# Layer 0 transposes x in 64-row halves, the condition's weights lead SP's queue, and the list run gets the trace's durations

## The chip, the cores and the metric

The kernel runs on one core of a Trainium2 chip. The metric is the device time of one execution in microseconds (us), lower is better. The kernel before takes 1091.3 us, the median of three runs (1090.01 to 1092.24). Engines are named as in the profile: PE is TensorE's matmul, PEld its weight load, DVE is VectorE, ACT is ScalarE, POOL is GpSimd, SP is the engine that issues most of the DMAs. A name with q (SPq, ACTq) is an engine's sequencer, which issues DMAs and waits.

## The reference, cut to what matters

x is 8 x 512 x 256, the condition 8 x 64, all in float32. Two layers follow each other; each batch element is independent of the others.

```python
# layer 0
scale = cond @ norm_w.T + 1.0
h = x * (scale[:, None, :] * rsqrt(mean(x * x, -1) + EPS))
val, gate = split(h @ up_w.T, 2, axis=-1)
h = val * gelu(gate)                      # 512 x 1024
hq = round-to-127-levels(h, per row);  wq = ternary(down_w)
x = hq @ wq.T + x
# layer 1, 16 heads of 16
x = x + a_alpha * attention(gamma * rmsnorm(x) + beta)
x = x + f_alpha * swiglu(gamma' * rmsnorm(x) + beta')
```

All `gamma`, `beta` and `alpha` are products of the condition with a weight of 256 x 64. They and `norm_w` are side by side in one array, `cond_w` (64 x 1792); its first 256 columns are `norm_w`.

## The kernel before, in words

Every step of the kernel is recorded as an operation of a plan: an engine, a cost in us, a function that emits the instructions, the values that it reads and writes, and a due time `at`. `Plan.order` then runs a list schedule: it keeps a clock for each engine, and whenever an engine is free it gives it the ready operation with the smallest due time. The order that comes out is the program order of every engine and of every DMA queue. So the costs written in the code decide which instruction stands ahead of which, and nothing else; on the chip an engine works through its order and waits on semaphores where it must. A DMA issued by ACT counts in the list as an ACT operation, whose result is there 0.12 us after its end; one issued by SP is there 2.5 us after its end.

PE operations have a mode: `full` (128 x 128), `rows` (two tiles of 64 rows, used side by side: scores, row maxima, the gated transposes of layer 1) and `columns` (four tiles of 32 columns, `quarters`, L383). A change of mode has a cost in the list, and rules keep modes together for a while. Values that need PSUM take one of 8 banks, or a pair of neighbours, from a named pool: `u` is banks 0 to 3 (results of the up matmuls), `fill` is 7, 5 and 6, `tp` the pairs (5,6), (2,3), (0,1). Pools may overlap; the list hands out the slot that has been free longest.

Order of the work: the start loads x of batch 0 in two halves (L390), the up weights in eight blocks of 256 KB (`load_up`, L403), and by ACT's queue the condition (`ct`) and `norm_w` (`nw`, both L394). POOL makes constants (L435 to L438) and fills `vts` and `thirds` (L456, L457). DVE makes `pick` in `constants2` (L443 to L446), which the scores need much later. PE multiplies `nw` by `ct` (L464), DVE adds 1 and writes it to `cvec` (L471): that is the value `scale`.

`norm0` (layer 0) squares x on ACT (L653), takes the root on POOL (L661, L662) and transposes x, not normalized, on PE. For batch 0 this goes in four pieces of two 128x128 transposes (`some`, L673), and the copy out of PSUM multiplies by `scale`, on ACT for the first 128 features (L678) and on DVE for the others (L680). For batches 1 to 7 there are two groups of four 128x128 transposes (L689), each into one `fill` bank, and two copies on ACT (L694). `up_tile` does 128 tokens: matmuls of 512 columns, two for each of four results (L710), GELU on ACT (L717), product on DVE (L744), the quantization (L756 to L779), a DMA transpose (L787), the down matmuls (L795) and the residual (L804).

Six batches of layer 0 go by themselves (to about 220 us); the last two are done in `columns` mode in between the attention of the first batches. Attention takes 128 steps of 5.8 us due time each: two score groups (L915, L917), exp on ACT (L948), row maxima for a later step (L932 on PE, L941 on DVE), weighted sums (L991), with projections and the swiglu of other batches (L383) in the gaps. `split` (L967 to L970) prepares the maxima for the scores. In layer 1 the normalized x before the swiglu is already transposed by halves: 16 transposes of 64 rows, two at a time, into a `tp` pair (`halves`, L581), and copied by L591.

Of the kernel before, what the change touches and what calls it, by code (L numbers as in the profile page):

```python
# [36 lines left out]
BF16 = mybir.dt.bfloat16  # L37
# [219 lines left out]
def act(n):  # L257
    return (n / 1.2 + 125) / 1e3


def dve(n):
    return (n / 0.96 + 115) / 1e3
# [11 lines left out]
def two_layers(ctx: ExitStack, tc: tile.TileContext, x, cond_t, cond_w, up_t, down_t, qkvo_t, gh_t, out_t, out_b, out):  # L274
# [109 lines left out]


# [11 lines left out]
    load("nw", lambda: mem(V["nw"])[:C, :D], cond_w[:, :D], -88, queue=se)  # L397
# [3 lines left out]
    def load_up(c, k):  # L401
        v = wup[c, k] = Val("wup")
        op("SP", dma(256), lambda: sp.dma_start(out=mem(v), in_=up_v[:, c, k * 512 : (k + 1) * 512]), writes=[v], at=-80)  # L403
# [49 lines left out]
    op("DVE", 2.0, constants2, writes=[V["pick"]], reads=[V["const"]], at=20)  # L453
# [24 lines left out]
    op("DVE", 0.2, lambda: condition_out(pn, 0, 1), reads=[pn], writes=[V["scale"]], at=-50)  # L478
    op("PE", 3.6, lambda: condition(pc, cw(), 1, 4), reads=[V["cw"], V["ct"]], writes=[pc], at=30)
# [52 lines left out]
    def norm(src, vsrc, scale, bias, name, at, step, pool="ht", gated=False):  # L532
# [10 lines left out]
        for t in range(NT):  # L543

            def square(t=t):
                if t == 0:
                    squares()
                ve.scalar_tensor_tensor(  # L548
                    mem(xn)[:, t * D : (t + 1) * D], in0=src()[:, t, :], scalar=1.0, in1=src()[:, t, :],
                    op0=ALU.mult, op1=ALU.mult, accum_out=ssq[0][:, t : t + 1],  # L550
                )

            op("DVE", 0.43, square, reads=[vsrc[t]], writes=[vs, xn], at=at)
# [9 lines left out]
        for t in range(NT):  # L563
            op(
                "DVE", 0.35,
                lambda t=t: ve.tensor_scalar(  # L566
                    mem(xn)[:, t * D : (t + 1) * D], src()[:, t, :], rstd[0][:, t : t + 1], None, op0=ALU.mult
                ),
                reads=[vs, vsrc[t]], writes=[xn], at=at + step,
            )  # L570
        ht = Val(pool)
        if gated:

            pt = Val("tp")

            def halves():
                for c in range(NC):
                    for t in range(NT):
                        for e in range(2):
                            r = slice(64 * e, 64 * e + 64)  # L580
                            pe.transpose(  # L581
                                mem(pt)[:, e, (c * NT + t) * 64 : (c * NT + t + 1) * 64],
                                mem(xn)[r, t * D + c * P : t * D + (c + 1) * P], ident[r, r],
                            )
# [3 lines left out]
            for c in range(NC):  # L588
                op(
                    "ACT", 0.65,  # L590
                    lambda c=c: se.activation(  # L591
                        mem(ht)[:, c * S : (c + 1) * S].rearrange("p (t e q) -> p t e q", t=NT, e=2),
                        mem(pt)[:, :, c * 256 : (c + 1) * 256].rearrange("p e (t q) -> p t e q", t=NT),
                        AF.Identity, bias=bias(c), scale=scale(c),
                    ),
                    reads=[pt, V["cvec"]], writes=[ht], at=at + (2 + c) * step,
                )
            return ht
        for c in range(NC):
            pt = Val("fill")  # L600

            def transposes(c=c, pt=pt):
# [9 lines left out]
                "ACT", 0.65,  # L612
# [33 lines left out]
    def norm0(b):  # L646
# [19 lines left out]
        for n in range(4 if b == 0 else 0):  # L666

            u, c = divmod(n, 2)
            pt = Val("fill")

            def some(u=u, c=c, pt=pt):
                for t in range(2):
                    pe.transpose(mem(pt)[:, t * P : (t + 1) * P], x1[:, b, 2 * u + t, c * P : (c + 1) * P], ident)  # L673

            def scaled(u=u, c=c, pt=pt):
                o, i, w = mem(ht)[:, c * S + u * 256 : c * S + u * 256 + 256], mem(pt)[:, :256], cvec[:, 0, c, b : b + 1]
# [5 lines left out]
            op("PE", 0.4, some, reads=[*vx1[b][2 * u : 2 * u + 2], V["const"]], writes=[pt], at=at + n * step, also=[ht])  # L682
            op(("ACT", "DVE")[c], act(256), scaled, reads=[pt, V["scale"]], writes=[pieces[u][c]], at=at + n * step, also=[ht])
        for c in range(NC if b else 0):
            pt = Val("fill")

            def transposes(c=c, pt=pt):
                for t in range(NT):
                    pe.transpose(mem(pt)[:, t * P : (t + 1) * P], x1[:, b, t, c * P : (c + 1) * P], ident)  # L689

            op("PE", 0.5, transposes, reads=[*vx1[b], V["const"]], writes=[pt], at=at + (2 + c) * step, also=[ht])
            op(
                "ACT", 0.65,
                lambda c=c, pt=pt: se.activation(  # L694
                    mem(ht)[:, c * S : (c + 1) * S], mem(pt), AF.Identity, scale=cvec[:, 0, c, b : b + 1]
# [5 lines left out]
    def up_tile(b, t, ht, at, late=False):  # L701
# [56 lines left out]
        def scales():  # L758
# [7 lines left out]
        op("DVE", 1.2, top, reads=[h], writes=[vst], at=a8)  # L766
        op("DVE", 0.6, scales, reads=[V["mean"]], writes=[vst], at=a8)
        op(
            "DVE", 0.7, lambda: ve.tensor_scalar(mem(h), mem(h), st["sc"], MAGIC, op0=ALU.mult, op1=ALU.add),
# [4 lines left out]
            "ACT", act(1024), lambda: se.activation(mem(q).bitcast(BF16), mem(h), AF.Identity, bias=magic),  # L774
# [3 lines left out]
            "DVE", 0.35,  # L778
# [12 lines left out]
        def down():  # L791
# [11 lines left out]
            "DVE", 0.42,  # L803
# [99 lines left out]
    def half_step(s, p):  # L903
# [4 lines left out]
        if now is not None:  # L908
# [3 lines left out]
            def scores():  # L912
# [10 lines left out]
                "PE", 0.43, scores, reads=[val["qk", n], vshift[n % 2], V["pick"]], writes=[sc], at=at, mode="rows",  # L923
# [28 lines left out]
    def shift(m):  # L952
# [19 lines left out]
        op("DVE", 0.5, split, reads=[vtop[k]], writes=[vthird[k]], at=at)  # L972
# [114 lines left out]
    def swiglu(b, at, first, place, stride=1.0):  # L1087
# [13 lines left out]
        for f in range(NF):  # L1101
            ps = []
            t, hid, gt = Val("t"), Val("hid"), Val("gt")
            for s in range(2):
# [22 lines left out]
                "DVE", dve(512) + 0.05,  # L1127
# [132 lines left out]
```

## Time and profile before

| what | value |
|---|---|
| median of three runs | 1091.3 us |
| the profiled execution: its time, its span | 1090.63 us, 1088.9 us |
| PE busy | 1065.4 us, 98% of the span |
| DVE, ACT, POOL busy | 631.7, 518.8, 205.7 us |
| granted TensorE clock, mean | 0.999 |
| DMA | 116.93 MB, mean 107 GB/s |
| four 128x128 transposes of L689, 48 of 56 before 215 us | 0.273 us each, pipelined |
| 16 half transposes of L581, x224 in all | 0.225 us each, pipelined |

The span is the time from the first to the last instruction of the profiled execution; the remainder of its time lies around it. A busy share of PE counts pipelined matmuls once, and their ends are modelled. In the timeline each line is: start, duration, engine, line of the code, operation, output and input, count, and in brackets the idle time before it with what ended it. In the waits each line is: who waited, for what, total us, how many times, the longest. In the windows each line is a stretch with the busy time and the number of instructions of PE, PEld, DVE, ACT and POOL, then the granted clock, the DMA share and GB/s.

### The profile page before, as it was taken

What the parts mean: (1) busy time and instruction counts of PE and PEld (TensorE: products, weight loads), DVE (VectorE), ACT (ScalarE), POOL (GpSimd) and SP (SyncE); (2) the same over time, 40 slices, a digit from 0 to 9 for tenths busy, and PEclk for the clock granted to TensorE, in tenths of its full rate; (3) what the DMA queues carried; (4) which work ended last, traced back from release to release, by engine and by line L of the source; (5) the groups of instructions that cost most, each with busy time, mean ns of one, the idle gap of its engine ahead of it and who ended that gap; (6) DMA issues with size and microseconds to landing.
All of it is one profiled execution on the core that took longest, in us unless ns stands there. A gap on an engine that the chain in (4) does not pass through costs nothing.

```text
span 1088.9 us, 22177 instructions
## 1 busy us (share of the span) xinstructions
PE 1065.4 (98%) x9336; PEld 442.9 (41%) x9336; DVE 631.7 (58%) x1044; ACT 518.8 (48%) x692; POOL 205.7 (19%) x198
## 2 busy tenths in 40 slices
PE   7999999999999999999999999999999999999998
PEld 4555454433333333433443344334333433342445
DVE  5665556876666854475557556654755474553131
ACT  3434433266666554455535544554455354436321
POOL 2100000000000321131123112311321132123242
PEclk9999999999999999999999999999999999999999
DMA  6322872124534542453254225514432452311100
GB/s 193 98 68 58 232 203 59 29 62 123 130 105 112 154 131 69 126 182 104 64 181 123 88 87 170 169 55 145 138 114 65 152 153 77 102 56 46 33 18 20
DMA packets 113828, 116.93 MB, mean 107 GB/s; under 512 B 59448, under 2 KB 69880, under 8 KB 113728
## 3 DMA queue, kind: packets, MB, share of 16 engines
q1 hardware_dynamic: 113568, 115.45, 36.5%
q8 instruction: 73, 1.20, 0.5%
q14 instruction: 27, 0.22, 0.1%
q10 hardware_dynamic: 160, 0.07, 0.0%
HBM read 56.49 MB, written 46.42 MB: 95 GB/s over the span
## 4 chain that ended last, share of the span: by engine, by line
PE 89%; DVE 5%; DMA 2%; ACT 2%; issue 1%; POOL 0%; ACTq 0%; SPq 0%; DVEq 0%
PE banks L383 40%; PE banks L710 15%; PE banks L991 9%; PE banks L915 6%; PE banks L932 5%; PE banks L917 4%; PE banks L1110 3%; DVE tops L941 2%; PE banks L795 2%; DMA a<-a 1%; PE banks L1151 1%; ACT a L948 1%; DMA aq<-hld 1%; DVE a L548 1%; DVE a L566 1%
## 5 line engine op out<-in xcount | busy, mean ns | idle before, releaser
L941 DVE TENSOR_REDUCE tops<-banks 128x2 f32<-128x1024 f32 x256 | 309.8, 1222 | 160.3 <-PE banks L932 158.8
L948 ACT ACTIVATE a<-banks 128x1024 f32<-128x1024 f32 x256 | 257.3, 1024 | 170.3 <-PE banks L917 152.9
L383 PE MATMUL banks<-a,gh 128*32 128x512 f32 x1792 | 208.2, 595 | 0.0
L710 PE MATMUL banks<-a,a 128*128 128x512 f32 x384 | 173.2, 599 | 0.4 <-DVE tops L941 0.4
L917 PE MATMUL banks<-aq 64*128 64x512 f32 x512 | 148.9, 577 | 0.0
L991 PE MATMUL banks<-a,vts 128*32 128x512 f32 x1024 | 135.1, 601 | 0.0
L1138 POOL TENSOR_TENSOR a<-a 128x512 f32<-128x512 f32 x64 | 81.8, 1278 | 256.8 <-ACT a L1134 248.6
L915 PE MATMUL banks<-shifts,pick 64*128 64x512 bf16 x512 | 101.2, 386 | 7.3 <-ACT a L948 5.1
L932 PE MATMUL banks<-aq 64*128 64x512 f32 x512 | 103.5, 417 | 4.4 <-ACT a L948 2.2
L383 PE MATMUL banks<-wout,a 128*32 128x256 f32 x1792 | 107.4, 381 | 0.0
L1128 DVE SCALAR_TENSOR_TENSOR a<-a,banks 128x512 f32<-128x512 f32 x64 | 44.0, 687 | 103.2 <-ACT a L1123 103.2
L710 PEld LDWEIGHTS banks<-a,a 128*128 128x128 f32 x384 | 71.2, 192 | 78.8 <-issue 73.5
L383 PEld LDWEIGHTS banks<-a,gh 128*32 128x32 f32 x1792 | 53.5, 109 | 119.7 <-issue 109.4
L915 PEld LDWEIGHTS <-pick 64*128 64x128 bf16 x512 | 26.8, 93 | 155.9 <-issue 150.8
L744 DVE SCALAR_TENSOR_TENSOR a<-banks,rstds,a 128x512 f32<-128x512 f32 x64 | 48.0, 750 | 68.4 <-PE banks L710 54.1
L717 ACT ACTIVATE a<-banks,rstds 128x512 f32<-128x512 f32 x64 | 43.4, 686 | 85.8 <-PE banks L710 83.0
L383 PEld LDWEIGHTS banks<-wout,a 128*32 128x32 f32 x1792 | 54.8, 110 | 52.9 <-issue 23.3
L1134 ACT ACTIVATE a<-banks 128x512 f32<-128x512 f32 x64 | 38.2, 597 | 73.5 <-PE banks L383 64.5
L1123 ACT ACTIVATE a<-banks 128x512 f32<-128x512 f32 x64 | 38.2, 597 | 63.2 <-PE banks L383 43.5
L1082 POOL TENSOR_TENSOR x<-x,a 128x512 f32<-128x512 f32 x31 | 40.2, 1298 | 138.7 <-DVE a L1073 132.5
L932 PEld LDWEIGHTS banks<-aq 64*128 64x128 f32 x512 | 48.7, 186 | 38.1 <-ACT a L948 12.0
L383 PE MATMUL banks<-a,a 128*32 128x512 f32 x512 | 59.3, 595 | 0.2 <-DVE a L744 0.2
(106 smaller groups left out, 945.2 us busy)
## 6 DMA issues: line engine op xcount, KB each, us to landing
hld<-a SPq DMA_DIRECT2D x128, 256.0 KB
aq<-hld SPq DMA_DIRECT2D x64, 512.0 KB
zd<-a SPq DMA_DIRECT2D x32, 256.0 KB
a<-zd SPq DMA_DIRECT2D x16, 256.0 KB
a<-rd SPq DMA_DIRECT2D x16, 256.0 KB
out_dram<-x SPq DMA_DIRECT2D x15, 256.0 KB
x<-in_x_dram SPq DMA_DIRECT2D x7, 512.0 KB
a<-in_up_t_dram SPq DMA_DIRECT2D x8, 256.0 KB
```

Source lines behind the costliest of these rows:

```text
L383: pe.matmul(o[32 * i : 32 * i + 32, :], w[:, 32 * i : 32 * i + 32], r, start=start, stop=stop)
L710: (quarters if late else pe.matmul)(mem(us[half, j]), mem(ht)[:, c * S + t * P : c * S + (t + 1) * P], mem(wup[c, 2 * half + j]), start=c ...
L717: se.activation(mem(gs[j]), mem(us[1, j]), AF.Gelu, scale=rstds[:, b, t : t + 1])
L744: lambda v=us[0, j], g=gs[j], j=j: ve.scalar_tensor_tensor(mem(h)[:, j * 512 : (j + 1) * 512], in0=mem(v), scalar=rstds[:, b, t : t + 1], ...
L915: pe.matmul(mem(sc)[:, e, :], pick[r, p, :], shifts[r, n % 2, :], start=True, stop=False)
L917: pe.matmul(mem(sc)[:, e, :], tile_of(n, 1, p, e)[:, kc * P : (kc + 1) * P], tile_of(n, 0, p, e), start=False, stop=True,)
L932: pe.matmul(mem(pm)[:, e, :], tile_of(m, 0, p, e)[:, qc * P : (qc + 1) * P], tile_of(m, 1, p, e), start=True, stop=True,)
L941: lambda: ve.tensor_reduce(tops[:, m % 2, 2 * p : 2 * p + 2, qc], mem(pm), AX.X, ALU.max, negate=True),
L948: lambda: se.activation(mem(e).rearrange("p (i s) -> p i s", i=2), mem(sc), AF.Exp, scale=0.25),
L991: pe.matmul(mem(pa)[32 * i : 32 * i + 32, :], vts[:, b % 2, kc, 8 * c + 4 * j + i, :], mem(es[i // 2])[:, (i % 2) * S : (i % 2 + 1) * S], ...
L1128: lambda t=t, i=ps[0]: ve.scalar_tensor_tensor(mem(t), in0=mem(t), scalar=1.0, in1=mem(i), op0=ALU.add, op1=ALU.mult),
L1138: "POOL", pool(512), lambda t=t, h=hid, g=gt: gp.tensor_tensor(mem(g), mem(t), mem(h), op=ALU.mult),
```

## The change

Three things are changed. First, `norm0` transposes x by halves: a helper `turn` makes two 64-row transposes of each 128x128 block, in mode `rows`, into a `tp` pair of banks; batches 1 to 7 get one group of 16 halves in place of two groups of four, and the copies read both banks with a rearranged pattern. Second, the start: `nw` is loaded by SP ahead of x, the up block (0, 2) by ACT in the place where `nw` was, and `constants2` now reads `scale`, so that it comes after L471. Third, the costs in the list: the formulas for ACT and DVE get 45 and 40 ns more, and a dozen single costs are set anew. The code that computes is not changed by the third.

```diff
 def act(n):
-    return (n / 1.2 + 125) / 1e3
+    return (n / 1.2 + 170) / 1e3
 def dve(n):
-    return (n / 0.96 + 115) / 1e3
+    return (n / 0.96 + 155) / 1e3
...
+    def turn(o, at, i):
+
+        for e in range(2):
+            r = slice(64 * e, 64 * e + 64)
+            pe.transpose(o[:, e, at : at + 64], i[r], ident[r, r])
...
-    load("nw", lambda: mem(V["nw"])[:C, :D], cond_w[:, :D], -88, queue=se)
+    load("nw", lambda: mem(V["nw"])[:C, :D], cond_w[:, :D], -95)
     load_x(0, -90, n=2)
...
-        op("SP", dma(256), lambda: sp.dma_start(out=mem(v), in_=up_v[:, c, k * 512 : (k + 1) * 512]), writes=[v], at=-80)
+        e, queue = ("ACT", se) if c == 0 and k == 2 else ("SP", sp)
+        op(e, 0.6 if e == "ACT" else dma(256), lambda: queue.dma_start(out=mem(v), in_=up_v[:, c, k * 512 : (k + 1) * 512]),
+           writes=[v], at=-88 if e == "ACT" else -80)
...
-    op("DVE", 2.0, constants2, writes=[V["pick"]], reads=[V["const"]], at=20)
...
     op("DVE", 0.2, lambda: condition_out(pn, 0, 1), reads=[pn], writes=[V["scale"]], at=-50)
+    op("DVE", 2.0, constants2, writes=[V["pick"]], reads=[V["const"], V["scale"]], at=20)
...
         for n in range(4 if b == 0 else 0):
             u, c = divmod(n, 2)
-            pt = Val("fill")
+            pt = Val("tp")
             def some(u=u, c=c, pt=pt):
                 for t in range(2):
-                    pe.transpose(mem(pt)[:, t * P : (t + 1) * P], x1[:, b, 2 * u + t, c * P : (c + 1) * P], ident)
+                    turn(mem(pt), t * 64, x1[:, b, 2 * u + t, c * P : (c + 1) * P])
...
-            op("PE", 0.4, some, ...)
+            op("PE", 0.2, some, ..., mode="rows")
...
-        for c in range(NC if b else 0):
-            pt = Val("fill")
-
-            def transposes(c=c, pt=pt):
+        if b == 0:
+            return ht
+        pt = Val("tp")
+
+        def halves():
+            for c in range(NC):
                 for t in range(NT):
-                    pe.transpose(mem(pt)[:, t * P : (t + 1) * P], x1[:, b, t, c * P : (c + 1) * P], ident)
+                    turn(mem(pt), (c * NT + t) * 64, x1[:, b, t, c * P : (c + 1) * P])
-            op("PE", 0.5, transposes, reads=[*vx1[b], V["const"]], writes=[pt], at=at + (2 + c) * step, also=[ht])
+        op("PE", 0.62, halves, reads=[*vx1[b], V["const"]], writes=[pt], at=at + 2 * step, also=[ht], mode="rows")
...
-            "DVE", 0.7, lambda: ve.tensor_scalar(mem(h), mem(h), st["sc"], MAGIC, op0=ALU.mult, op1=ALU.add),
+            "DVE", 0.98, lambda: ve.tensor_scalar(mem(h), mem(h), st["sc"], MAGIC, op0=ALU.mult, op1=ALU.add),
...
-                "PE", 0.43, scores, reads=[val["qk", n], vshift[n % 2], V["pick"]], writes=[sc], at=at, mode="rows",
+                "PE", 0.455, scores, reads=[val["qk", n], vshift[n % 2], V["pick"]], writes=[sc], at=at, mode="rows",
...
-        op("DVE", 0.5, split, reads=[vtop[k]], writes=[vthird[k]], at=at)
+        op("DVE", 0.95, split, reads=[vtop[k]], writes=[vthird[k]], at=at)
```

The other new costs: the squares of `norm` 0.43 to 0.47, its products 0.35 to 0.4, the row maximum of a tile (L756) 1.2 to 1.22, the rounding on ACT (L774) 0.1 more, the clipping (L779) 0.35 to 0.42, the residual (L804) 0.42 to 0.48, the ACT copies after transposes 0.65 to 0.77, and the swiglu's product (L1128) loses 0.05 that it had on top of the formula. `halves` of layer 1 is written with `turn` and stays as it was.

## The prediction

> **What bounds the kernel now.** I read the page first, its busy shares and its chain of work.
>
> ```profile
> span 1088.9 us, 22177 instructions
> PE 1065.4 (98%) x9336; PEld 442.9 (41%) x9336; DVE 631.7 (58%) x1044; ACT 518.8 (48%) x692; POOL 205.7 (19%) x198
> PE 89%; DVE 5%; DMA 2%; ACT 2%; issue 1%; POOL 0%; ACTq 0%; SPq 0%; DVEq 0%
> ```
>
> TensorE (PE) has 98% and 89% of the chain; nobody else comes near. What shortens the time is a shorter PE step or a shorter PE wait. Next come the stages of the run (columns: busy time of PE, PEld, DVE, ACT, POOL, then granted clock, DMA share, GB/s).
>
> ```profile
> 13.00:220.00 207.00, 206.28 (x685) 102.58 (x684) 133.06 (x262) 80.69 (x140) 12.07 (x16) 1.00 0.43 107
> 220.00:1010.00 790.00, 777.61 (x8099) 295.64 (x8101) 474.41 (x741) 416.88 (x514) 160.28 (x143) 1.00 0.38 113
> ```
>
> Layer 0 leaves PE idle for 0.7 us of 207, attention for 12.4 of 790. Third, the timeline of the start.
>
> ```profile
> 0.72 0.97 SPq L390 DMA_DIRECT2D x<-in_x_dram  x2
> 1.30 0.61 ACTq L394 DMA_DIRECT2D a<-in_cond_w_dram  x1
> 2.04 4.08 DVE L446 TENSOR_SCALAR pick<-ones,pair 128x128 bf16<-128x128 f32 x1
> 5.51 0.52 POOL L457 MEMSET thirds<- 128x512 bf16 x1
> 6.11 0.99 PE L464 MATMUL banks<-ct,a 64*128 64x8 f32 x4 [6.11 <-DMA a<-in_cond_w_dram]
> 7.03 1.97 PE L673 MATMUL banks<-ident,x 128*128 128x128 f32 x8
> 8.79 15.64 PE L710 MATMUL banks<-a,a 128*128 128x512 f32 x32
> 10.50 0.34 PEld L710 LDWEIGHTS banks<-a,a 128*128 128x128 f32 x1 [0.52 <-issue]
> 12.68 0.19 PEld L710 LDWEIGHTS banks<-a,a 128*128 128x128 f32 x1 [0.24 <-issue]
> ```
>
> PE does nothing until 6.11: its first work is the condition (L464), and its weights, issued second on ACT's queue at 1.30, land only then. The transposes of x stand behind it in PE's order, though ACT already reads x's first half at 3.78. The first up matmul starts at 8.79; its weight loads come 0.85 us apart until 12.2 and 0.43 apart from then on: the clock is half until there.
>
> **The change, part by part**, summed against the profiled execution's own 1090.63 us (span 1088.9 and 1.7 around it); the median of the runs shown is 1091.3, so 0.7 above it.
>
> *Start.* The condition's weights (64 KB) go to the head of SP's queue, and x's two halves and seven up blocks move back by one issue there (0.43 to 0.5 us each); one up block goes to ACT's queue in the weights' old place, so ACT issues as much as before. x's first half, four times as large, is issued at 0.72 and read at 3.78; so the weights are there by 3.8 at the latest. The four condition matmuls took 0.92 (6.11 to 7.03): done at 4.7, and `scale` by DVE (0.17) at 4.9. x's first half, one issue later, lands near 4.3; its transposes run on the cold clock (0.22 for each 128x128: 8 from 7.03 to 8.79), and half tiles run two at a time, so about 0.5: done at 5.2, ACT's copy (0.47) at 5.7.
> DVE has the other half of the pieces, and here the moved `constants2` matters. It now reads `scale`, so it can start at 4.9; the list has it ready at once, while the pieces still wait for x, so I expect it ahead of them. Its first L446 ran 4.08 us and ended at 6.12, 0.09 after POOL's last memset (6.03): I take it that it can't end before 6.1 after the change either. The second pair (0.15 + 0.29) ends at 6.6, DVE's first piece (0.48) at 7.1. That piece feeds the second matmul of the first up group, now at 9.64 (8.79 + 0.85). Upper bound of the gain: 9.64 - 7.1 - 0.1 = 2.4 us. The next late thing is the up weights: in the trace's semaphore events the fourth load of 256 KB is complete at 7.93, and the same bytes are ahead of it afterwards; by that the gain is 1.7. If the clock still doubles at 12.2, the time won is spent on cold matmuls (0.85 for 0.43) and half stays, 0.9. The pieces now take pairs of banks, two of them up banks, so the first up group also waits until ACT has read the third piece: x's second half near 5.0, transposed by 5.5, two squares (0.4 each) and the copy, 6.3; earlier than the DVE piece. No loss follows from any of these rows, so the ends are 0 and -2.4. I take **-1.6**, nearest to the weights' landing.
> The row for the clock is the spacing above: 3.4 us of up matmuls until it doubles. The Trainium skill (TensorE: Matmul & The Clock Gate, Part 1) says that a busy window of about 3.4 us, free-running, opens the clock; by that an earlier start is an earlier fast clock and the term stays whole, give or take a window in single runs.
>
> *Transposes, batches 1 to 7.* Each has two groups of four 128x128 transposes now, then one group of 16 in 64-row tiles, in pairs. Layer 1 has this form already, at L581.
>
> ```profile
> 95.97 0.60 PE L689 MATMUL banks<-ident,x 128*128 128x128 f32 x4
> 96.41 3.60 PE L710 MATMUL banks<-a,a 128*128 128x512 f32 x8
> 99.84 1.04 PE L604 MATMUL banks<-ident,a 128*128 128x128 f32 x8
> ```
> ```profile
> 217.50 3.70 PE L710 MATMUL banks<-a,a 128*128 128x512 f32 x8
> 221.13 0.71 PE L581 MATMUL banks<-ident,a 64*128 64x64 f32 x16
> 221.67 0.38 PE L915 MATMUL banks<-shifts,pick 64*128 64x512 bf16 x2
> ...
> 227.91 0.40 PE L932 MATMUL banks<-aq 64*128 64x512 f32 x2
> 228.24 1.06 PE L991 MATMUL banks<-a,vts 128*32 128x512 f32 x8
> ```
>
> A step is the distance of starts, since durations overlap. Four transposes: 0.44; a batch's two groups 0.88. Sixteen halves: 221.13 to 221.67, 0.54. But the array's shape changes on both sides. Eight up matmuls between equals take 3.43 (96.41 to 99.84); those at 217.50, behind 64-row work and ahead of it, 3.63: so 0.20 for the entry into rows and the first full matmul after rows. Leaving costs the last pair 0.10 (0.33 at 227.91, where a pair inside a run takes 0.23 on the chain). Among up matmuls a batch thus costs 0.54 + 0.20 + 0.10 = 0.84 for 0.88: five batches, -0.2. Batches 6 and 7 stand among 64-row work already (188.5 and 222.5 to 227.5): there the switch goes too; 0.88 becomes 0.54, and about as much again for the switch of one of them, together -0.8. Sum **-1.0**. ACT's copies of halves are longer (L591 0.774, L694 0.685), 14 x 0.09 = 1.2 us of ACT, which is busy for 81 of 207 us: nothing. The new form needs two neighbouring PSUM banks at once. (5,6) are hardly used in layer 0; if the list took two of the up tiles' four banks, PE would wait for at most the two copies, 1.5 us a batch: 6 x 1.5 = +9 is the far end, the near one -1.0 - 0.6.
> Against this part speaks the Trainium skill (TensorEngine Tiling (Array Packing), Key Properties): changing the tiling mode drains TensorE. It gives no price; by the rule alone five batches would lose. The rows show the drain, 0.30 a round trip, and the pairs pay for it.
>
> *The list's durations.* No instruction changes, but the order on all engines is worked out anew. The large ones: exp 0.978 to 1.023 (L948 runs 1.024), row maxima 1.182 to 1.222 (L941 1.222), scores 0.43 to 0.455, splits 0.5 to 0.95 (four instructions, 0.97). One moves away: the scaling at L769 goes from 0.7 to 0.98 and runs 0.75. What can be won is PE waiting behind work that the list thought done earlier. The waits of attention (us, times, longest):
>
> ```profile
> PE banks L915 <- ACT a L948: 5.1, 5, 2.1
> PE banks L932 <- ACT a L948: 2.2, 6, 0.4
> PE banks L915 <- DVE tops L941: 1.7, 5, 0.4
> ```
>
> With the weight loads' waits, PE stands behind L948 or L941 48 times there. Each was 0.04 to 0.045 too early: 48 x 0.045 = 2.2, and I take half, since an order that avoids one wait often makes another: **-1.1**. The ends: all of PE's idle 12.4 gone, and on the other side more changes of shape. I count 218 returns from 64-row work in PE's records; entry and exit cost 0.19 to 0.30. A tenth more rounds is 22 x 0.2 = +4.4.
>
> **Sum**: 1090.63 - 1.6 - 1.0 - 1.1 = 1086.9; from the median it would be 1087.6. I say **1087.0**.
>
> **Rivals.** About 0.2% (2.2 us) is what a measurement of this kernel can tell from no change.
> (1) *Forecast*: start and transposes pay, the order is neutral to slightly better: 1083 to 1089, 0.50.
> (2) *The order gains much*: the waits behind L948 and L941 (9.6 us on PE itself in attention) mostly go: 1086.9 - 5 = 1082, reaching 1079. For it: these waits; against: the list's error is only 4%, and the waits of 1 to 2 us at 222.9 and 250 follow table loads on ACT (1.28), which no duration here changes. 0.16.
> (3) *The start is hidden*: up weights or clock take back the gain, or the change does not do what it says (DVE's first piece waits for `constants2` and POOL's memsets as long as it waited for the condition, or the durations move away as at L769): with -0.5 to -1 for the transposes, 1089.1 to 1092. 0.21.
> (4) *Slower*: the new order changes PE's shape more often. It decides when the added rounds eat the 3.7 us and 2.2 more: 5.9 / 0.2 = 30 more than 218. Then 1093.5 to 1097. For it: the longer scores and maxima can break up runs of 64-row work; against: the rules of batching are untouched. 0.13.
>
> Faster by over 0.2%: (1) and (2), 0.66; within: 0.21; slower: 0.13. The range leaves out the far part of (2) and (4): 1081 to 1093.
>
> **What would show it.** Start: condition before 4.8, L446 ending near 6.1, first up matmul between 6.2 and 8, its second before 8.3. Wrong if DVE's piece comes after 8. Transposes: 16 halves in 0.54, next up matmul within 0.7; wrong if PE waits at them for a bank. Order: PE idle in 220 to 1010 below 12 us and no more than about 218 rounds; a count beyond 240 would mean (4).

## The result, and the profile after

The changed kernel takes 1105.5 us (median of four runs, 1104.43 to 1106.4); the kernel before, in the same session, 1091.7 (median of four, 1090.01 to 1092.24). The ratio is 1.0129 with an interval of [1.0111, 1.0146]: 13.8 us slower, where I had said 4 us faster and given "slower" 0.13. The profiled execution took 1104.69 us (before 1090.63). From here on, L numbers are those of the kernel that a line is from; in the changed kernel the lines of attention stand 8 further down (L915 becomes L923, L932 L940, L941 L949, L948 L956), L710 is L718, and all half transposes are issued in `turn`, L389.

The page of the changed kernel, span, busy shares and chain:

```profile
span 1102.9 us, 22312 instructions
PE 1068.7 (97%) x9400; PEld 441.7 (40%) x9400; DVE 631.2 (57%) x1044; ACT 519.4 (47%) x692; POOL 205.3 (19%) x198
PE 89%; DMA 4%; DVE 3%; ACT 2%; issue 1%; SPq 1%; POOL 0%; DVEq 0%; ACTq 0%
```

PE is still the only engine that matters. It is busy for 3.3 us more in a span that is 14.0 longer, so most of the loss is PE waiting. The windows of the two stages (columns as in the prediction):

```profile
13.00:220.00 207.00, 205.83 (x732) 100.31 (x731) 134.29 (x261) 80.33 (x139) 11.52 (x16) 1.00 0.44 108
220.00:1010.00 790.00, 767.13 (x7986) 292.97 (x7988) 475.00 (x740) 410.59 (x504) 156.56 (x140) 1.00 0.39 113
```

Layer 0 is as full as before (1.2 us idle for 0.7). In attention PE idles 22.9 us for 12.4, and it gets through 8099 - 7986 = 113 matmuls fewer in the same 790 us. The first score of attention comes at 221.18 us in the trace (221.67 before), the last at 1021.7 (1008.0 before); what follows is as long as it was (81.2 us for 80.9). From first to last score it takes 800.5 us for 786.3. So the whole loss lies between the first and the last score. The waits of PE in the changed kernel:

```profile
PE banks L923 <- ACT a L956: 8.2, 9, 2.6
PE banks L923 <- DVE tops L949: 5.3, 8, 1.3
...
PE banks L389 <- ACT a L956: 2.8, 3, 0.9
PE banks L940 <- DVE tops L949: 1.7, 3, 0.9
...
PE banks L940 <- ACT a L956: 1.5, 4, 0.5
PE banks L718 <- DVE tops L949: 0.7, 1, 0.7
```

Against the same view of before: scores (L923) waited 5.1 us for exp and 1.7 for the row maxima, now 8.2 and 5.3; half transposes of layer 1 that stand directly behind a group of scores now wait for exp too (2.8 us), which none did. I call **W** the sum of all waits of PE behind exp or row maxima in this view. In before's view these are the three lines that the prediction shows and two more:

```profile
PE banks L932 <- DVE tops L941: 0.6, 1, 0.6
...
PE banks L710 <- DVE tops L941: 0.4, 1, 0.4
```

W is 10.0 us before and 20.2 after: 10.2 of the 14.0 us between the spans of the two profiles.

The longest one is the first of attention. ScalarE, then PE, at that place in the changed kernel's timeline, and PE's wait there before:

```profile
221.62 0.76 ACT L593 ACTIVATE a<-banks,cvec 128x512 f32<-128x512 f32 x1
222.39 1.28 ACT L956 ACT_TABLE_LOAD   x1
223.69 1.02 ACT L956 ACTIVATE a<-banks 128x1024 f32<-128x1024 f32 x1
```
```profile
221.63 0.49 PE L940 MATMUL banks<-aq 64*128 64x512 f32 x2
224.76 0.39 PE L923 MATMUL banks<-shifts,pick 64*128 64x512 bf16 x2 [2.65 <-ACT a L956]
```
```profile
225.25 0.39 PE L915 MATMUL banks<-shifts,pick 64*128 64x512 bf16 x2 [2.06 <-ACT a L948]
```

A copy stands ahead of exp on ACT, exp needs its table first, and PE has nothing else in its order until the exp has read its banks. Then PE comes back with the clock at half for a while. The same 8 us, before and after:

```profile
224.00:228.00 4.00, 2.75 (x24) 1.98 (x23) 2.63 (x7) 3.99 (x11) 0.00 (x0) 1.00 0.00 0
228.00:232.00 4.00, 4.00 (x40) 1.20 (x40) 3.27 (x11) 3.96 (x5) 2.04 (x4) 1.00 0.13 26
```
```profile
224.00:228.00 4.00, 3.18 (x18) 0.99 (x21) 2.24 (x6) 3.74 (x7) 0.00 (x0) 0.76 0.00 0
228.00:232.00 4.00, 4.00 (x30) 1.46 (x26) 1.36 (x4) 2.08 (x7) 1.20 (x2) 0.82 0.00 0
```

4 x 0.24 + 4 x 0.18 = 1.7 us lost to the clock. With W that makes 11.9 of the 14.0; the remaining 2.1 I can't assign to a row.

The start of the changed kernel:

```profile
0.72 0.59 SPq L400 DMA_DIRECT2D a<-in_cond_w_dram  x1
1.31 0.60 ACTq L410 DMA_DIRECT2D a<-in_up_t_dram  x1
1.37 1.32 SPq L396 DMA_DIRECT2D x<-in_x_dram  x2
3.54 0.99 PE L471 MATMUL banks<-ct,a 64*128 64x8 f32 x4 [3.54 <-DMA a<-in_cond_w_dram]
5.03 1.09 DVE L454 TENSOR_SCALAR pick<-ones,pair 128x128 bf16<-128x128 f32 x1
6.11 0.42 ACT L655 ACTIVATE a<-x 128x256 f32<-128x256 f32 x1 [2.67 <-DMA x<-in_x_dram]
6.22 1.68 PE L389 MATMUL banks<-ident,x 64*128 64x64 f32 x16 [1.69 <-DMA x<-in_x_dram]
6.95 0.48 DVE L683 TENSOR_SCALAR a<-banks,cvec 128x256 f32<-128x256 f32 x1 [0.33 <-PE banks L389]
8.19 1.22 PE L718 MATMUL banks<-a,a 128*128 128x512 f32 x1 [0.28 <-ACT a L681]
```

The condition is done at 4.5 for 7.0, but x's first half, read by ACT at 3.78 before, is there only at 6.1, and the first up matmul begins at 8.19 for 8.79.

### The profile page after: what moved, and what is told of

It is laid out like the page before. It is cut to its first block, busy times and chain, and to the rows that moved or that the text cites. A ratio compares the mean times of both kernels' runs of the same rounds, so it can differ in the third digit from the quotient of the medians.

```text
span 1102.9 us, 22312 instructions
## 1 busy us (share of the span) xinstructions
PE 1068.7 (97%) x9400; PEld 441.7 (40%) x9400; DVE 631.2 (57%) x1044; ACT 519.4 (47%) x692; POOL 205.3 (19%) x198
## 4 chain that ended last, share of the span: by engine, by line
PE 89%; DMA 4%; DVE 3%; ACT 2%; issue 1%; SPq 1%; POOL 0%; DVEq 0%; ACTq 0%
PE banks L383 39%; PE banks L718 15%; PE banks L999 10%; PE banks L923 6%; PE banks L940 6%; PE banks L925 4%; PE banks L1118 3%; PE banks L803 2%; ACT a L956 1%; DMA a<-a 1%; PE banks L1159 1%; DVE tops L949 1%; PE banks L389 1%; DMA als<-ald 1%; DMA aq<-hld 1%
## 5 line engine op out<-in xcount | busy, mean ns | idle before, releaser
L949 DVE TENSOR_REDUCE tops<-banks 128x2 f32<-128x1024 f32 x256 | 309.4, 1221 | 157.4 <-PE banks L940 155.5
L956 ACT ACTIVATE a<-banks 128x1024 f32<-128x1024 f32 x256 | 257.5, 1024 | 177.8 <-PE banks L925 149.7
L718 PE MATMUL banks<-a,a 128*128 128x512 f32 x384 | 174.0, 600 | 1.0 <-DVE tops L949 0.7
L925 PE MATMUL banks<-aq 64*128 64x512 f32 x512 | 149.2, 577 | 0.0
L923 PE MATMUL banks<-shifts,pick 64*128 64x512 bf16 x512 | 100.9, 386 | 14.5 <-ACT a L956 8.2
L940 PE MATMUL banks<-aq 64*128 64x512 f32 x512 | 105.8, 418 | 5.4 <-DVE tops L949 1.7
L718 PEld LDWEIGHTS banks<-a,a 128*128 128x128 f32 x384 | 70.8, 191 | 80.1 <-issue 72.9
L923 PEld LDWEIGHTS <-pick 64*128 64x128 bf16 x512 | 27.0, 93 | 162.0 <-issue 158.1
L940 PEld LDWEIGHTS banks<-aq 64*128 64x128 f32 x512 | 49.8, 186 | 43.6 <-issue 10.3
```

Of the source, the lines that this page charges most:

```text
L718: (quarters if late else pe.matmul)(mem(us[half, j]), mem(ht)[:, c * S + t * P : c * S + (t + 1) * P], mem(wup[c, 2 * half + j]), start=c ...
L923: pe.matmul(mem(sc)[:, e, :], pick[r, p, :], shifts[r, n % 2, :], start=True, stop=False)
L925: pe.matmul(mem(sc)[:, e, :], tile_of(n, 1, p, e)[:, kc * P : (kc + 1) * P], tile_of(n, 0, p, e), start=False, stop=True,)
L940: pe.matmul(mem(pm)[:, e, :], tile_of(m, 0, p, e)[:, qc * P : (qc + 1) * P], tile_of(m, 1, p, e), start=True, stop=True,)
L949: lambda: ve.tensor_reduce(tops[:, m % 2, 2 * p : 2 * p + 2, qc], mem(pm), AX.X, ALU.max, negate=True),
L956: lambda: se.activation(mem(e).rearrange("p (i s) -> p i s", i=2), mem(sc), AF.Exp, scale=0.25),
```

## The experiments

Seventeen kernels were run, none of which leaves out any of the computation. Times are medians; "before" was 1090.2 to 1092.1 in the five sessions. All are in one table at the end of this section, with the W of each one's profile.

**First, the parts.** Which of the three edits loses the time: the durations, the halves, the start, or only all of them together? The expectations number the theories.

`e1_durations`: before, with all new costs of the list and nothing else.

> The kernel before with all the new durations in the list, and with the old start and the old transposes. Theory 1 (the durations make an order in which PE waits longer in attention): the whole loss of 13.8 us is here, 1102 to 1107. Theory 2 (the halves do it: the one group of 16 at the border of attention needs a bank pair, PE waits 2.7 us there and the clock falls for 3.4 us, and the order behind it is another one): 1089 to 1094 here. Theory 3 (the sum of the parts, none of which has more than half): 1096 to 1099.

1102.4 (+10.7), in theory 1's range. The code that computes is before's; what differs is the order of the instructions, and with it the slots, since the list also hands out banks and buffers. "Order" stands for both from here on; no run takes them apart.

`e2_no_durations`: the changed kernel with the old costs.

> The changed kernel with the old durations: the new start and the halves stay. Theory 1: 1087 to 1092, level with the kernel before or a little faster. Theory 2: 1100 to 1106, the loss stays. Theory 3: 1096 to 1100.

1098.5 (+6.8), in theory 3's range: so the durations are not all of it.

`e3_start`: before, with the new start only (`nw` first on SP, the up block on ACT's queue, `constants2` behind `scale`).

> The kernel before with the new start alone: the condition's weights first on SP, one up block on ACT's queue, constants2 behind the scale. In the changed kernel that up block landed ahead of x (5.35 against 6.09 for x's first half, which was there at 3.76 before), so the first up matmul came at 8.19 in place of 8.79. All theories: 1090 to 1092; by my prediction's sum 1.6 us would be won, 1090. Over 1094 would mean that the order of the later work hangs on the start.

1089.6 (-2.1), ratio 0.9983 [0.9973, 0.9994]. It is the only part that gains, and alone it beats both kernels. How much of the 2.1 the start's own steps earned is not shown. Its later work has another order: the first score comes at 224.69 us for 221.67 and W is 8.8 for 10.0. And the clock was kinder to it: 8 of its 10 executions had a mean granted clock of 0.999 or 1.000, 7 of 13 of before in that session; the medians of these alone are 1089.5 and 1090.8.

`e4_halves`: before, with the half transposes only.

> The kernel before with the transposes by halves alone, old durations and old start. Theory 1: 1089 to 1092 (my prediction has -1.0 for it). Theory 2: 1100 to 1106, with PE waiting over 2.5 us for ACT near 222 and a lower clock for about 3.4 us behind it. Theory 3: 1094 to 1097.

1098.7 (+7.0), between the ranges of theories 3 and 2. The parts give -2.1 + 10.7 + 7.0 = 15.6 for 13.8 together: two parts lose, each by itself.

**Second, whether it is the numbers or the re-made order.** Theory A: each list is a draw, and any disturbance of it moves the time by microseconds; B: the halves cost by themselves; C: the larger formulas are bad numbers; D: recorded durations overcharge the engines, and steps from start to start would be right.

`e5_halves_due`: `e4_halves` with the group's due time 2 us later in the list.

```diff
-        op("PE", 0.62, halves, ..., at=at + 2 * step, also=[ht], mode="rows")
+        op("PE", 0.62, halves, ..., at=at + 2 * step + 2, also=[ht], mode="rows")
```

> The halves-only kernel (1098.7) with the due time of the one group of 16 moved 2 us later, into the middle of the due times of the two old groups; the instructions are the same. Theory A (the halves themselves cost nothing; the loss is the order that the list falls into, where PE waits behind exp and row maxima in attention): 1088 to 1093, most of the 7 us gone by a due time alone. Rival B (the form costs it: 64-row tiles among full matmuls, two banks held at once, slower copies): 1097 to 1100 as before.

1094.9 (+3.6): half of the loss gone by a due time. That lies between A's range and B's.

`e6_halves_mode7`: `e4_halves`, but the list takes batch 7's group for `full`; the instructions are the same.

```diff
-        op("PE", 0.62, halves, ..., mode="rows")
+        op("PE", 0.62, halves, ..., mode="full" if b == B - 1 else "rows")
```

> The halves-only kernel with one word changed in the list: the group of batch 7, the only one of them that stands in attention, counts as full and not as rows. PE executes the same 16 half transposes. Theory A: the loss hangs on that place in the order, 1090 to 1095. Rival B: 1097 to 1100, since all instructions stay.

1095.3 (+4.0), just above A's range: again some 3 us, by a remark to the list about one group.

`e7_formulas`: before, with the two formulas alone (170 for 125, 155 for 115).

> The kernel before with the two formulas for ACT and DVE alone at the new values (45 and 40 ns more for every such operation), the single durations old. Theory A (no single number is to blame, every disturbed list comes out some us worse than this one): 1092 to 1098, part of the 10.7 us of all durations. Theory C (the formulas are to blame, since exp and row maxima go through them): 1100 to 1104. If the single numbers are to blame: 1090 to 1092.

1098.6 (+7.3), between A's range and C's.

`e8_steps`: before, with steps read off back-to-back operations of its trace in place of durations (exp 0.920 for a recorded 1.024, row maxima 1.137 for 1.222, scores 0.455, splits 0.81, ...) and larger latencies (ACT 0.2, DVE 0.18).

> The kernel before with durations that are the distance of starts of operations that follow each other without a gap in the trace, and not the recorded durations, which overlap: exp 0.92 (recorded 1.024), row maximum 1.137 (1.222), 512 elements on DVE 0.603 (0.69), the scaling 0.665 (0.745); what is taken off is put on the list's latencies (0.08 more for ACT and DVE). Theory D (the trace's durations overcharge the engines by 0.08 to 0.1 for each operation, and the list works against engines that are fuller on paper than on the chip): 1085 to 1092, no loss or a gain. Theory A: 1093 to 1100, another order, no better for being nearer to the chip.

1096.0 (+4.7), A's range. Steps are less bad than durations by 6 us, but a list with better numbers is still worse than the one before. D holds in part at most.

`e9_two_ns` and `e10_ten_ns`: before, with the formulas at 127 and 117, and at 135 and 125.

> The kernel before with 2 ns more in each of the list run's two formulas (127 and 117 for 125 and 115); every instruction is the same, only their order can change. Theory A (the time is set by how each order happens to place PE's waits inside 64-row work, and any change of the numbers draws another order): 2 to 7 us slower than before or, with less chance, up to 3 us faster, so outside plus or minus 0.5 us. Theory C (the larger formulas are worse numbers, in proportion to their size: 45 ns cost 7.2 us): 2 ns cost 0.3 us, within 0.5 us of before. Theory D (recorded durations overcharge by 0.085 to 0.1 us): also within 0.5 us.

> The kernel before with 10 ns more in each of the two formulas (135 and 125); every instruction the same. Theory C and D (loss in proportion to the overcharge): 10 of 42 ns of a loss of 7.2 us is 1.7 us slower than before. Theory A: no relation to the size; it may be anywhere from 3 us faster to 7 us slower, and above all not between the times of the 2 ns and the 45 ns kernel except by chance. A time under that of before, or one over that of the 45 ns kernel, speaks for A.

2 ns cost 4.6 us (ratio 1.0042 [1.0028, 1.0056]), 10 ns cost nothing (1.0007 [0.9993, 1.002]). No price per nanosecond does that. The waits of the 2 ns kernel:

```profile
PE banks L915 <- ACT a L948: 5.5, 6, 2.1
PE banks L915 <- DVE tops L941: 3.2, 8, 1.0
PE banks L932 <- ACT a L948: 2.8, 7, 0.5
PE banks L932 <- DVE tops L941: 2.4, 3, 1.2
```

and of the 10 ns kernel:

```profile
PE banks L915 <- ACT a L948: 5.1, 5, 2.1
PE banks L932 <- ACT a L948: 2.2, 6, 0.4
PE banks L915 <- DVE tops L941: 1.9, 6, 0.4
...
PE banks L932 <- DVE tops L941: 0.6, 1, 0.6
```

With 0.4 in a further line of each (L710 behind L941), W is 14.3 and 10.2, for 10.0 before: the differences, 4.3 and 0.2, are close to those of the times, 4.6 and 0.1.

**Third, the start's queue.** `e11_up_on_sp`: `e3_start`, but all up blocks stay on SP's queue.

> The kernel before with the condition's weights first on SP's queue and the second constants behind the scale, but with all up blocks on SP's queue behind x, as before; the block on ACT's queue is left out of the start. Theory U (that block, 256 KB issued at 1.3 us and landed at 5.35, held x's first half back to 6.09, which landed at 5.1 or earlier without it): x lands before 5.2, the first transposes of x begin before 5.6 and the first up matmul before 7.6, against 7.79 with the block on ACT's queue; total equal to that start's 1089.6 or up to 0.6 us under it. Theory V (x is late because of the weights ahead of it on its own queue, and the up block is needed early): x lands near 6.1 all the same, the first up matmul waits for its block until 8.5 or later, total 0.5 to 1.5 us over that start's 1089.6.

Its timeline of PE:

```profile
3.27 0.99 PE L463 MATMUL banks<-ct,a 64*128 64x8 f32 x4 [3.27 <-DMA a<-in_cond_w_dram]
4.63 1.08 PE L673 MATMUL banks<-ident,x 128*128 128x128 f32 x4 [0.37 <-DMA x<-in_x_dram]
7.17 2.56 PE L710 MATMUL banks<-a,a 128*128 128x512 f32 x3
```

U is right on the mechanism: without the block on ACT's queue x's first half is there at 4.5 (5.95 in `e3_start`, 6.1 in the changed kernel), and the first up matmul starts at 7.17. On the time it is wrong, as V is: 1091.5, ratio 0.9995 [0.9984, 1.0006], which `e3_start`'s interval overlaps. Of the 0.62 us that the first up matmul gains on `e3_start` (7.79) little is left further on: the second up matmul starts at 8.2 for 8.6 in `e3_start`, the third at 9.0 for 9.2, the ninth at 11.7 for 11.8. The clock doubled at 9.22 in this profile and at 8.97 in that one, so how much the later weights and pieces have to do with it is not shown. Its median is 1.9 above that of `e3_start`; most of that goes with the clock. The six of its twelve executions with a mean granted clock of 0.999 or 1.000 have a median of 1089.8 (1089.5 for the eight of `e3_start`), the other six 1092.1. Its profiled execution took 1088.0, less than any other profiled one here.

**Fourth, order or instructions, draw or price.** `e12_list_of_halves`: the list of `e4_halves`, so the same order, but each group of 16 halves is emitted as 8 full transposes.

```diff
-                    turn(mem(pt), (c * NT + t) * 64, x1[:, b, t, c * P : (c + 1) * P])
+                    pe.transpose(mem(pt)[:, c, t * P : (t + 1) * P], x1[:, b, t, c * P : (c + 1) * P], ident)
```

> The kernel with the halves alone, its list run and so its order unchanged to the last instruction, but in layer 0 each group of 16 halves is emitted as 8 full 128-row transposes again, as before. Theory A (the halves cost nothing themselves, the order that the list makes for them does): the loss of 7.0 us stays, 1097 to 1101, a little more than with halves being possible because a full batch takes 0.88 us for 0.54 and, in attention, leaves the 64-row mode. Theory B (the halves as instructions cost the time): with the instructions of before the loss goes, 1091 to 1093.

1101.7 (+11.5). The loss does not go away with the halves: the order costs it. Whether the halves save anything in that order is not shown: the ratios, 1.0105 and 1.0072, are apart by 0.33% (3.6 us) with an interval of about 0.3, and some 1.7 us of that are a clock at half, which this kernel's profile has near 230 us and that of `e4_halves` doesn't.

`e13_durations_minus` and `e14_durations_plus`: `e1_durations` with the formulas at 168 and 153, and at 172 and 157.

> The kernel before with all of the new durations, but the two formulas 2 ns lower (168 and 153). Theory A in its pure form (every set of numbers draws an order, and 10.7 us is a bad draw): the time moves by 2 us or more from the 1102.4 of the exact durations, either way. Theory C (the durations as such are worse numbers by some 10 us): it stays within 1.5 us of 1102.4.

> As the last, with the formulas 2 ns higher than the trace's durations (172 and 157). Pure A: again 2 us or more from 1102.4, and not the same as with 2 ns less. C: within 1.5 us of 1102.4. If both neighbours stay over 1098 though they differ, both hold: the new durations shift the draws upward, and single numbers scatter them.

1101.1 and 1101.5. The second turned out to have the order of `e1_durations` to the last instruction, so it is a repeat (1101.5 against 1102.4) and no draw. The first has another order and, within 1.3 us, the same loss: C's range. So 10.7 is not the bad luck of a single order, as far as one neighbour can tell.

`e15_single_durations`, `e16_act_formula`, `e17_dve_formula`: before, with the new costs other than the formulas; with ScalarE's formula alone; with VectorE's alone.

> The kernel before with all of the new durations but the two formulas (13 lines of the list). Theory C (each wrong number has its own price, and prices add): 10.7 us for all less 7.2 for the formulas is 3.5 us slower than before. Theory A2 (any re-made list loses some us, and once it is re-made more changes add little or take back): 5 to 11 us slower, so that the two parts together come to clearly more than the 10.7 of both.

> The kernel before with ScalarE's formula alone at 170 for 125. Theory C: this and VectorE's formula alone add up to the 7.2 us of both. If ScalarE's overcharge is the one to blame, all of it is here (the waits behind exp grew most); A2: 3 to 8 us here and as much in the other, together well over 7.2.

> The kernel before with VectorE's formula alone at 155 for 115. C: what is left of 7.2 us after ScalarE's part. A2: 3 to 8 us by itself.

1099.5 (+7.4), 1093.6 (+1.5) and 1098.3 (+6.2), ratios 1.0060, 1.0021 and 1.0044. The two theories share these results. The formulas apart, 0.21 + 0.44 = 0.65%, give what they give together (0.73%), and 1.5 us is under A2's range: C's pattern. But the single durations cost 7.4 us, where C said 3.5 and A2 5 to 11, and with the formulas together that makes 0.60 + 0.73 = 1.33% for the 1.04 and, repeated, 1.05% of both: A2's pattern, though the difference of 0.3% is no larger than its interval. So what stands is that every list with much larger costs lost time, and that a tiny change can cost 4.6 us; whether prices add up is open.

The table: all kernels in the order of W.

| kernel | us | ratio, interval | span of the profiled run | W |
|---|---|---|---|---|
| e16_act_formula | 1093.6 | 1.0021 [1.0008, 1.0034] | 1091.2 | 7.8 |
| e3_start | 1089.6 | 0.9983 [0.9973, 0.9994] | 1087.7 | 8.8 |
| e11_up_on_sp | 1091.5 | 0.9995 [0.9984, 1.0006] | 1086.2 | 9.0 |
| before | 1091.7 | | 1088.9 | 10.0 |
| e10_ten_ns | 1092.0 | 1.0007 [0.9993, 1.0020] | 1089.3 | 10.2 |
| e8_steps | 1096.0 | 1.0040 [1.0027, 1.0053] | 1094.3 | 10.7 |
| e6_halves_mode7 | 1095.3 | 1.0041 [1.0026, 1.0055] | 1093.5 | 11.1 |
| e5_halves_due | 1094.9 | 1.0031 [1.0018, 1.0044] | 1094.5 | 11.4 |
| e7_formulas | 1098.6 | 1.0073 [1.0055, 1.0091] | 1095.2 | 12.6 |
| e12_list_of_halves | 1101.7 | 1.0105 [1.0090, 1.0120] | 1100.0 | 13.3 |
| e2_no_durations | 1098.5 | 1.0065 [1.0041, 1.0088] | 1095.5 | 13.5 |
| e4_halves | 1098.7 | 1.0072 [1.0045, 1.0099] | 1095.1 | 14.1 |
| e9_two_ns | 1096.5 | 1.0042 [1.0028, 1.0056] | 1093.2 | 14.3 |
| e17_dve_formula | 1098.3 | 1.0044 [1.0030, 1.0058] | 1097.0 | 15.3 |
| e13_durations_minus | 1101.1 | 1.0095 [1.0078, 1.0113] | 1098.5 | 15.9 |
| e15_single_durations | 1099.5 | 1.0060 [1.0042, 1.0078] | 1098.6 | 15.9 |
| e1_durations | 1102.4 | 1.0104 [1.0081, 1.0128] | 1101.1 | 17.0 |
| e14_durations_plus | 1101.5 | 1.0105 [1.0089, 1.0121] | 1102.2 | 17.1 |
| the changed kernel | 1105.5 | 1.0129 [1.0111, 1.0146] | 1102.9 | 20.2 |

Over these 19 profiles the span rises with W (correlation 0.89, 1.3 us for 1 us of W). W is not the whole story (`e8_steps` loses 4.7 us at 0.7 more W), but no other group of PE's waits follows the time like this: for those behind DMAs after the start the correlation is 0.28, for those behind other work of ACT, DVE and POOL 0.04.

## Why the prediction was wrong, point by point

*The list's durations (-1.1, ends -12.4 to +4.4): this step failed.* They cost 10.7 us by themselves. I had taken 48 waits (the two views of before have 50), each 0.04 to 0.045 us too early in the list, and given half of that as gain. Three things were wrong in it.

First, the waits were not too early. In before's trace PE goes on 1.076 us after the start of the exp that it waited for, and 1.276 after that of the row maximum (medians of its 17 such waits in attention). The list before had 0.978 + 0.12 = 1.098 and 1.182 + 0.10 = 1.282, cost and latency: right to 0.02 us. With the recorded durations it has 1.143 and 1.322, so 0.07 and 0.05 too late. And it charges the engine 1.023 and 1.222 for steps of 0.920 and 1.137. The prediction says itself, of PE, that a step is the distance of starts; for ACT and DVE it took the durations.

Second, the working treats the order as fixed and lets each operation slide by its own error; but the list makes a new order, and `e9_two_ns` shows that 2 ns in the formulas move the time by 4.6 us.

Third, nothing in the reckoning said that the list before was an ordinary one, which truer numbers would improve. Of the fifteen kernels here with other costs, due times, modes or pools in the list (all but the two of the start; thirteen different orders), fourteen were slower, by 1.5 to 11.5 us, and one the same: among its neighbours the order before is a good one. My far end, +4.4, came from changes of shape and was far too near.

The list has a clock of its own, which could have been read beforehand: `Plan.order`, run alone on the recorded kernels, ends at 1074.4 us for before, 1096.2 for the changed kernel, 1094.7 for `e1_durations`, 1079.4 for `e4_halves`, 1077.0 with 2 ns, 1074.5 with 10 ns and 1073.7 for `e3_start`. Over the 19 kernels these ends follow the measured ratios with a correlation of 0.84. It is no sure guide (`e5_halves_due` ends at 1073.1 and was slower), and it doesn't say why, but it had the sign of each of the three parts.

*Transposes (-1.0, ends +9 and -1.6): right as instructions in layer 0, wrong as an edit; the second step that failed.* In layer 0 the timeline of the changed kernel has

```profile
87.05 3.60 PE L718 MATMUL banks<-a,a 128*128 128x512 f32 x8
90.58 0.71 PE L389 MATMUL banks<-ident,x 64*128 64x64 f32 x16
91.22 1.98 PE L718 MATMUL banks<-a,a 128*128 128x512 f32 x4
93.04 1.04 PE L803 MATMUL banks<-a 128*128 128x256 bf16 x8
```

Eight up matmuls ahead of the group take 3.53 for 3.43, the group 0.64 until the next up matmul, the four behind it 1.82 where four between equals take 1.72 (99.94 to 101.66 in the same trace): 0.64 + 0.10 + 0.10 = 0.84, the number of the prediction, for 0.88. All six groups that stand ahead of up matmuls take 0.64 to the next one. (For the other two batches the prediction's own terms, twice 0.34 and one switch of 0.30, give -1.0 and not -0.8; only one of them, batch 7, stands in attention now.) PE waits for no bank there, so the far end of +9 had the wrong reason. But the group has another mode, pool and cost in the list. With that list the kernel loses 7.0 us with halves (`e4_halves`) and 11.5 without them (`e12_list_of_halves`), so the loss is the order's; 4.1 us of it are W (14.1 for 10.0). I counted the edit's instructions and not the order that it leads to.

*Start (-1.6): right in sign; the size is partly luck.* Alone it gave -2.1, but with another order behind it and more executions at full clock, as said. The condition was done at 4.5 (4.7 said), L454's first ended at 6.12 (6.1 said), DVE's first piece at 7.43 (7.1 said). Wrong was x: I had its first half near 4.3, and it came at 6.1, because the up block on ACT's queue, issued at 1.31, went ahead of it; `e11_up_on_sp` shows x at 4.5 without that block. I had priced this block at nothing, as ACT issues no more than before; I did not count what it does to the transfers of the other queue. The first up matmul at 8.19 was then 0.2 behind the bound that I had set, and it waited for ACT's third piece, which I had at 6.3 and which ended at 8.13; the second came at 9.20, where I had said before 8.3. Nor is the moment when the clock doubles fixed, as the sum had it (12.2): in the eleven profiles with the old start and the old transposes it lies between 9.8 and 13.0, and the ninth up matmul starts between 12.5 and 14.8 (13.96 before). In the three with the whole new start the ninth starts at 11.8, 13.1 and 13.2. So one profile against one can't weigh this start to better than a microsecond or two.

*Rival (4)* had the sign and not the mechanism. It needed 30 more rounds of shape; PE's records show 450 changes of mode for 444, three rounds more, and `e1_durations`, which lost 10.7 us, has 437. What grew is PE standing inside its 64-row work, in nearly the same number of rounds. The check that I had named (PE idle below 12 us in 220 to 1010) did tell: it was 22.9.

What is shown: that the loss is in the order (with the slots that go with it) and not in the instructions (`e1_durations`, `e7_formulas`, `e9_two_ns` and `e13_durations_minus` have before's instructions; `e12_list_of_halves` keeps the order and the loss), that it lies between the first and the last score, and that W makes up 10.2 of the 14.0 us between the profiles. What stays open: why orders from the larger costs have more W in a regular way; that the list thinks ACT and DVE fuller than they are is a guess at it. That recorded durations overcharge is measured, but the list with steps (`e8_steps`) was slower too, with little W, and I have no row for its 4.7 us. An order that is before's by hand with the halves put in was not tried; whether the halves pay there is open as well.

## What to carry to other kernels

Where a schedule is computed from costs in the code, an edit of a cost, a mode, a pool or a due time is an edit of the whole order: price it as a new draw among orders (here 4.6 us slower to 0.1 for 2 and 10 ns), not as a shift of the operations that it names, and be wary where the present draw is a good one. Read the list's own end before the run: it is free, and here it had the sign of each part. Take costs as steps from start to start, and check the time at which a waiting engine goes on, before calling a number of the list wrong. Truer costs do not make a better list by themselves. Measure each part of such a change alone, and disturb a cost by a hair to learn how wide the draws lie before a gain of 1 us is believed. Compare executions of equal granted clock.

## What the runs showed of the hardware

*A recorded duration is longer than the engine's step.* In the changed kernel's timeline of ScalarE:

```profile
226.67 1.02 ACT L956 ACTIVATE a<-banks 128x1024 f32<-128x1024 f32 x1 [0.17 <-PE banks L925]
227.59 0.41 ACT L655 ACTIVATE a<-x 128x256 f32<-128x256 f32 x1
```

The next operation starts 0.92 after an exp that is recorded with 1.02. In before's trace, operations that start before the one ahead has ended show the same: exp goes 0.920 from start to start for 1.024 recorded, the row maxima 1.137 for 1.222. The overlap is 0.09 to 0.11 us for most lines of ScalarE that wait for nothing and 0.07 to 0.09 for most of VectorE.

*The clock falls by windows of 3.41 us, not by the length of a pause.* Pauses of 2.65 us near 222 to 228 us were followed by 3.41 us at half clock in the changed kernel, `e2_no_durations` and `e12_list_of_halves`, while those of 2.64 and 2.65 in `e4_halves` and `e6_halves_mode7` were not. After 2.06 it fell in `e15_single_durations` and `e17_dve_formula` and not in five others, before among them; after 1.96 it fell in `e1_durations` and `e14_durations_plus`. Each fall costs half of 3.41, so 1.7 us. In the traces' records of the clock the stretches at full clock are whole multiples of 3.413 us (215.04 is 63 of them, 873.81 is 256, 1075.20 is 315). Laid out in such windows from the moment of its doubling, the window ahead of each of these seven falls has PE idle for 1.71 to 2.39 us in sum, and in the twelve profiles without a fall before 1075 us no window until then has more than 1.71. So what decides is how much of a pause lies in one window, with the border near half of it. PE's ends are modelled, and one fall does not fit: a second one in `e17_dve_formula`, at 371.7 us, has 1.29 ahead of it. The same kernel can therefore fall in one execution and not in the next: of 72 executions of before, the 43 with a mean granted clock of 0.999 or 1.000 took 1090.7 us on average, the 27 with 0.998 took 1092.6.

*A transfer on another queue delays one that was issued beside it.* x's first half (256 KB), issued at 1.36 on SP's queue, was read by ACT at 5.95 in `e3_start`, with a 256 KB block issued at 1.31 on ACT's queue; issued at 1.37 without that block, it was read at 4.52 (`e11_up_on_sp`).
